# The head of full attention in a macaron block: query scale in the row masks, expert sums between the first scores, keys and values as jobs beside the first maxima

## The chip, the cores and the metric

The kernel runs on one core of a Trainium2 chip. The metric is the device time of one execution in microseconds. TensorE is called PE (PEld for its weight loads), VectorE DVE, ScalarE ACT, GpSimd POOL, SyncE SP. All data are fp32.

## The reference

Two "macaron" layers run one after the other on x of shape (2, 2048, 256), each as half a feed-forward block, attention, and half a feed-forward block, each with a layer norm in front:

```python
x = x + 0.5 * experts(layernorm(x))
x = x + attention0(layernorm(x))        # full: q = x@Wq.T * (1/16), 16 heads of 16
x = x + 0.5 * experts(layernorm(x))
x = x + 0.5 * recurrence(layernorm(x))
x = x + attention1(layernorm(x))        # causal, rotary, relative positions; q / 4
x = x + 0.5 * recurrence(layernorm(x))
```

`experts` sends each token to the 2 best of 6 experts (gated feed-forward blocks), adds the two results with their weights, and adds a shared block of the same form. `attention0` ends with `out @ Wff.T + bff`.

## The kernel before, in words

x (4096 tokens of 256) stays in SBUF as 32 chunks of 128 tokens; batch 0 is chunks 0 to 15, batch 1 chunks 16 to 31. The order of every engine's work is that of the program; nothing is reordered by a scheduler. PSUM is a ring of eight banks (`bank()`), taken in the order of the program by all products, so a product waits until whoever read the bank eight allocations before has done so.

**The expert stage** (`moe`) routes and sorts each batch's tokens, scatters them to DRAM (`places`) in the order of their experts, and runs the experts over tiles of 128 rows (`experts`), which go to DRAM again (`results`). Then `combine(h, c)` brings chunk c of batch h together: for each of the token's two experts POOL issues an indirect gather from `results` into a buffer `yg` (L435), and DVE multiplies it with its weight and adds it to x (L440, a scalar_tensor_tensor with two SBUF inputs). The sums of batch 0 are made while the experts run for batch 1. Those of batch 1 (16 chunks, 32 gathers and 32 sums) follow the experts, through `rest(n)`: n chunks at a time between the last products of the shared block (`up`, `mul`, `down`; L145, L336, L343). In the first expert stage no pool `gathered` is given: `yg` has 6 buffers in the stage's own pool, and `rest(HC)` makes all remaining sums before the stage ends. In the second it lies in a pool of its own with 12 buffers, and the remaining sums are called from `recurrence`.

**Full attention** (`attention0`) has 32 groups t of one batch, one block of 512 queries and 4 heads. The four heads of a group lie in rows 32j to 32j + 15 of the partitions, or, for odd groups, in rows 32j + 16 to 32j + 31. `queries(t)` makes one product for two groups and writes it twice, through `part_rows` (L138): an ACT activation whose scale is a column of the table `rowsel`, 1 in the rows that count and 0 in the others. `keys(b, g, qc)` does the same for the keys of two groups and one block of 512, with a bias column besides. `vals` makes the values of 8 heads for 512 keys (16 matmuls of 128 columns, L603, and an ACT copy, L609), after two small ACT writes that pad them (L620, L624).

`largest` computes 128 x 512 scores of one head (L757) and DVE takes their maximum per row (L761); 64 of these per group, then `mneg` (L764) holds the negative maxima. `subtract` puts them into the query's spare row. `exponential` computes scores turned over (L771), with ACT's Exp (L776). `weighted` multiplies them with the values (L783), four products per unit, which ACT copies out (L643) and POOL adds up (L541).

**The order around the change.** A step has two half steps, n = 0 and 1. A half step has 4 exponentials of one group interleaved with 4 maxima of a later group, then its half of the step's jobs, then one unit of `weighted`. Exponentials begin in step 9; in steps 0 to 7 only the first group's maxima run, in step 8 the second's first ones. Jobs are listed by step in `jobs`: `queries(0)` is due at step -2; at step -1 stand four `add_bias` (POOL adds the output bias to x of batch 0 in 128 x 1024 pieces, L587), the eight `keys` of batch 0's first and third group pairs, and its eight `vals`. Before any of these the attention scales the query weights with 1/16 on DVE (L721), and POOL clears two tiles (`mneg`, L555). In the later `recurrence` a similar DVE instruction scales the query weights of `attention1` with 1/4.

Of the kernel before, what the change touches and what calls it, by code (L numbers as in the profile page):

```python
# [17 lines left out]
P = 128  # L18
B = 2
S = 2048  # L20
D = 256
# [21 lines left out]
def macaron_kernel(ctx: ExitStack, tc: tile.TileContext, t: dict, out: bass.AP):  # L43
# [6 lines left out]
    nc.gpsimd.memset(mhalf, -0.5)  # L50


    rowsel = const.tile([P, 4], F32, name="rowsel")


    xpool = ctx.enter_context(tc.tile_pool(name="xpool", bufs=1))
# [109 lines left out]
    def moe(w, ws, gate_w, gate_b, rev, tri, iota, z, behind, last, gathered):  # L166
# [3 lines left out]
        with ExitStack() as s:  # L170
# [257 lines left out]
            def combine(h, c):  # L428

                for i in range(2):  # L430
                    yg = (wk if gathered is None else gathered).tile(
                        [P, D], F32, name="yg", bufs=6 if gathered is None else 12
                    )
                    k = i * HC + c
                    nc.gpsimd.indirect_dma_start(  # L435
                        out=yg, out_offset=None, in_=results[h],
                        in_offset=bass.IndirectOffsetOnAxis(ap=place[h][:, k : k + 1], axis=0),
                    )
                    xs = x[:, h * HC + c, :]
                    nc.vector.scalar_tensor_tensor(  # L440
                        xs, yg, weight[h][i][:, c, :], xs, ALU.mult, ALU.add
                    )
# [260 lines left out]
                skew.append(u)  # L703


    def attention0(norm, tail, wq, wk_, wv, wo, bff):

        with ExitStack() as s:
            z = Pieces(s, "a0", norm, wo, bff)
            kpool = pool(s, "a0_k", side="right")
            vpool = pool(s, "a0_v", side="right")
            wk, q = z.wk, z.q
            groups = [(b, qc, g) for b in range(B) for qc in range(SB) for g in range(G)]

            nc.vector.tensor_scalar_mul(wq, wq, 1.0 / 16.0)  # L721
            NG = len(groups)
            kT, v, mx = {}, {}, {}

            def keys(b, g, qc):

                pk = bank()
                mm2(pk, wk_, ts(g // 2, P), z.xnT(b, qc))
                for i in range(2):
                    if qc == 0:  # L730
                        kT[b, g + i] = kpool.tile([P, S], F32, name="kT", bufs=5)
                    part_rows(kT[b, g + i][:, ts(qc, TB)], pk, i, rowsel[:, 2 + i : 3 + i])

            vs = [vpool.tile([P, NKB, HV * VW + DH - 1], F32, name=f"v{n}") for n in range(3)]

            def vals(b, half, qc):
                if qc == 0:
                    v[b, half] = vs[(2 * b + half) % 3]
                if 2 * b + half < 3:
                    z.pad_values(vs[2 * b + half][:, ts(qc, CPB), :])  # L740
                z.values(v[b, half][:, ts(qc, CPB), :], wv, b, qc, half, None)

            def queries(t):

                b, qc, g = groups[t]
                pq = bank()
                mm2(pq, wq, ts(g // 2, P), z.xnT(b, qc))
                for i in range(2):
                    q[t + i] = wk.tile([P, TB], F32, name="q", bufs=4)
                    part_rows(q[t + i], pq, i, None)  # L750
                    mx[t + i] = wk.tile([P, CPB * J, SB], F32, name="mx", bufs=4)

            def largest(t, u, j):
                b, qc, g = groups[t]
                qb, kc = u // SB, u % SB
                ps = bank()
                nc.tensor.matmul(  # L757
                    ps, lhsT=q[t][rows(j), ts(qb, P)], rhs=kT[b, g][rows(j), ts(kc, TB)],
                    start=True, stop=True,
                )  # L760
                nc.vector.tensor_reduce(mx[t][:, qb * J + j, kc : kc + 1], ps, AX.X, ALU.max)  # L761
                if u == NKB - 1 and j == last_j:
                    m = z.mnegs[t % 2].rearrange("p a j r -> p (a j) r")
                    nc.vector.tensor_reduce(  # L764
                        m[:, :, z.row(t)], mx[t], AX.X, ALU.max, negate=True
                    )

            def exponential(t, kb, j):
                b, qc, g = groups[t]
                st = bank()  # L770
                nc.tensor.matmul(  # L771
                    st, lhsT=kT[b, g][rows(j), ts(kb, P)], rhs=q[t][rows(j), :],
                    start=True, stop=True,
                )
                z.pTs[t, kb, j] = wk.tile([P, TB], F32, name="pT", bufs=8)
                nc.scalar.activation(z.pTs[t, kb, j], st, AF.Exp)  # L776

            def weighted(t, kb):
                b, qc, g = groups[t]
                pv = bank()  # L780
                for j in range(J):
                    h = (g % 2) * J + j
                    nc.tensor.matmul(  # L783
                        pv[rows(j), :], lhsT=v[b, g // 2][:, kb, ds(h * VW, 32)],
                        rhs=z.pTs.pop((t, kb, j)), start=True, stop=True,
                    )
                z.gather(t, pv, 4)

            jobs = Jobs()
            at = jobs.at  # L790
            PER = 8
            for t in range(NG):
                at(PER * t + 8, z.subtract, t)
            for b in range(B):
                first = b * SB * G * PER

                for qc in range(SB) if b else ():
                    for c in range(CPB):
                        at(first - 43 + 4 * qc + c, z.ln_stats, b, qc, c)
                    at(first - 37 + 4 * qc, z.ln_transpose, b, qc)  # L800
                for qc in range(0 if b else SB):
                    norm.xn.pop(qc)
                    at(-1, z.add_bias, qc)
                for g in range(0, G, 2):
                    for qc in range(SB):
                        at(first - 7 + PER * g + qc if b else -1, keys, b, g, qc)
                for half in range(2):
                    for qc in range(SB):
                        due = first + 1 + 16 * half + qc
                        at(due if b else -1, vals, b, half, qc)  # L810
            for t, (b, qc, g) in enumerate(groups):
                if t % 2 == 0:
                    at(PER * t - 2, queries, t)
                at(PER * t + 18, z.divide, t, b, qc, g, True)
                if g == G - 1:
                    at(PER * t + 19, z.outputs_T, b, qc)
                    at(PER * t + 20, z.outputs, b, qc, 0)
                    at(PER * t + 20, z.outputs, b, qc, 1)

            at(60, fill_skew)  # L820
            for step, fn, *args in tail:
                at(PER * NG + step, fn, *args)
            for step in range(min(jobs), max(jobs) + 1):
                todo = jobs.get(step, [])
                for n in range(2):
                    z.begin(2 * step + n)
                    te, tm = (step - 9) // PER, step // PER
                    ke, um = ((step - 9) % PER) * 2 + n, (step % PER) * 2 + n
                    exps = 0 <= te < NG
                    last_j = 1 if exps else 3  # L830
                    for j in range(J):
                        if exps:
                            exponential(te, ke, j)
                        if 0 <= tm < NG:
                            largest(tm, um, (j + 2) % J if exps else j)
                    for fn, args in todo[n * (len(todo) + 1) // 2 :][: (len(todo) + 1 - n) // 2]:
                        fn(*args)
                    unit = 2 * (step - 9) + n - 1
                    if 0 <= unit < NG * NKB:
                        weighted(unit // NKB, unit % NKB)  # L840
            z.finish()
# [136 lines left out]
    def attention1(norm, tail, w, relk, relv, kbias, dramp, skew):  # L978
# [4 lines left out]
        with ExitStack() as s:  # L983
# [85 lines left out]

            def queries_out(t):  # L1070
                for i in range(2):
                    part_rows(q[t + i], q[t + 1], i, None)

            def by_position(t):

# [353 lines left out]
    with tc.manual_schedule(engines=ENGINES):  # L1429

        n0, n1, n2, n3, n4, n5 = (Norm() for _ in range(6))
        with ExitStack() as s:
# [9 lines left out]
            def loads0():  # L1442
                weights.extend(load(wp, n) for n in ("a0_q", "a0_k", "a0_v", "a0_o", "a0_b"))

            run_moe(n0, ahead.run, nothing, loads0, clear=True)
            tail = []
            for b in range(3):
                tail += [(1 + 2 * b, n2.stats, b), (2 + 2 * b, n2.normal, b, nc.vector),
                         (3 + 2 * b, n2.turn, b)]
            tail.append((7, n2.stats, 3))  # L1450
            attention0(n1, tail, *weights)


        with ExitStack() as s:
# [25 lines left out]
            def normals(cb):  # L1480

                if cb == 1:


                    nc.vector.tensor_scalar_mul(a["q"], a["q"], 0.25)
                    nc.vector.scalar_tensor_tensor(
                        kbias, rowsel[:, 0:2], rel0[:, 0:1], rowsel[:, 2:4], ALU.mult, ALU.add
                    )
# [22 lines left out]
def _layout(i):  # L1511
# [52 lines left out]

    rowsel = np.zeros((J, 2, DH, 4), f)
    for n in range(2):
        rowsel[:, n, :, n] = 1.0
        rowsel[:, 1 - n, 0, 2 + n] = 1.0  # L1570
    o["rowsel"] = rowsel.reshape(P, 4)
    o["rev"] = np.broadcast_to(np.arange(NE, 0, -1, dtype=f), (P, 1, NE))
    inv = (f(1.0) / f(10000.0) ** (np.arange(0, DH, 2, dtype=f) / f(DH))).astype(f)
    ang = np.outer(np.arange(S, dtype=f), inv).astype(f)
# [24 lines left out]
```

## Time and profile before

| what | value |
|---|---|
| median of 3 runs | 4118.79 us (4115.33 to 4121.76) |
| profiled execution, its own time | 4118.51 us |
| its span, first to last instruction | 4116.6 us |
| mean granted PE clock | 0.985 |
| PE busy | 4012.2 us, 97% of the span |
| DVE busy | 2702.9 us, 66% |
| ACT busy | 2570.1 us, 62% |
| POOL busy | 1634.7 us, 40% |
| gathers `yg<-results`, L435 | 128, 0.94 us each on POOL, data 2.8 us after issue (median) |
| sums `x<-yg`, L440 | 128, 0.48 us each (median), longest 9.84 us |
| maxima `mx<-s`, L761 | 2048, 0.68 us each |

A row of the timeline gives start, length, engine, line, operation and, in brackets, the idle time before it with what ended it. In rows of stretches, busy times of the engines are followed by the granted PE clock, as a share of full speed. "x" counts records; an fp32 matmul leaves two. Times of overlapping instructions are longer than their spacing: the maxima follow each other closer than 0.68 us apart.

### The profile page before, as it was taken

What the parts mean: (1) busy time and instruction counts of PE and PEld (TensorE: products, weight loads), DVE (VectorE), ACT (ScalarE), POOL (GpSimd) and SP (SyncE); (2) the same over time, 40 slices, a digit from 0 to 9 for tenths busy, and PEclk for the clock granted to TensorE, in tenths of its full rate; (3) what the DMA queues carried; (4) which work ended last, traced back from release to release, by engine and by line L of the source; (5) the groups of instructions that cost most, each with busy time, mean ns of one, the idle gap of its engine ahead of it and who ended that gap; (6) DMA issues with size and microseconds to landing.
All of it is one profiled execution on the core that took longest, in us unless ns stands there. A gap on an engine that the chain in (4) does not pass through costs nothing.

```text
span 4116.6 us, 76431 instructions
## 1 busy us (share of the span) xinstructions
PE 4012.2 (97%) x28256; PEld 1950.3 (47%) x28256; DVE 2702.9 (66%) x6130; ACT 2570.1 (62%) x5227; POOL 1634.7 (40%) x1456
## 2 busy tenths in 40 slices
PE   8996999999999999999999999999999999999999
PEld 4664533333334433333345654655554455554445
DVE  6243888888776788888843344666677756677533
ACT  2332488888887888888853322266667766667832
POOL 4244133336433333333344240245546655554410
PEclk9998899999999999999999999999999999999999
DMA  7341000100000000000023420154442334442101
GB/s 258 116 128 54 1 1 1 47 1 1 1 1 1 1 1 1 1 1 1 10 85 130 128 86 6 37 119 91 98 96 56 84 78 90 101 91 53 45 22 41
DMA packets 355508, 223.18 MB, mean 54 GB/s; under 512 B 146624, under 2 KB 338496, under 8 KB 355136
## 3 DMA queue, kind: packets, MB, share of 16 engines
q1 hardware_dynamic: 276800, 176.33, 16.3%
q0 software_dynamic: 12288, 33.57, 2.6%
q10 hardware_dynamic: 66048, 8.39, 1.3%
q8 instruction: 225, 3.69, 0.4%
q14 instruction: 147, 1.20, 0.1%
HBM read 113.12 MB, written 105.12 MB: 53 GB/s over the span
## 4 chain that ended last, share of the span: by engine, by line
PE 90%; DVE 5%; POOL 2%; ACT 1%; issue 1%; DMA 1%; SPq 0%; POOLq 0%; DVEq 0%; ACTq 0%
PE s L771 13%; PE s L783 12%; PE s L757 10%; PE s L145 10%; PE s L1236 7%; PE s L382 6%; PE s L1122 6%; PE s L1207 6%; PE s L402 3%; PE s L680 1%; PE s L603 1%; PE s L1221 1%; PE s L1200 1%; PE s L343 1%; PE s L1217 1%
## 5 line engine op out<-in xcount | busy, mean ns | idle before, releaser
L541 POOL TENSOR_TENSOR part<-part 128x512 f32<-128x512 f32 (+3 forms) x800 | 962.8, 1204 | 1436.3 <-ACT part L643 1428.2
L761 DVE TENSOR_REDUCE mx<-s 128x1 f32<-128x512 f32 x2048 | 1270.1, 683 | 327.4 <-PE s L757 327.2
L776 ACT ACTIVATE pT<-s 128x512 f32<-128x512 f32 x2048 | 1063.7, 617 | 236.5 <-PE s L757 234.5
L757 PE MATMUL s<-kT,q 32*128 32x512 f32 x4096 | 1033.6, 630 | 0.0
L771 PE MATMUL s<-q,kT 32*128 32x512 f32 x4096 | 1013.3, 615 | 0.0
L1228 ACT ACTIVATE pT<-s 128x512 f32<-128x512 f32 (+3 forms) x1280 | 587.5, 541 | 252.1 <-PE s L1207 103.9
L771 PEld LDWEIGHTS s<-q,kT 32*128 32x128 f32 x4096 | 417.8, 183 | 465.9 <-DVE mx L761 327.0
L643 ACT COPY part<-s 128x512 f32<-128x512 f32 (+3 forms) x864 | 507.0, 588 | 148.9 <-PE s L783 60.1
L1130 DVE TENSOR_REDUCE mx<-s 128x1 f32<-128x512 f32 (+1 forms) x768 | 472.9, 679 | 131.1 <-PE s L1122 122.7
L783 PE MATMUL s<-pT,v 128*32 128x512 f32 x4096 | 549.8, 605 | 0.4 <-ACT pT L776 0.2
L757 PEld LDWEIGHTS s<-kT,q 32*128 32x128 f32 x4096 | 426.1, 187 | 127.5 <-ACT pT L776 76.5
L1122 PE MATMUL s<-kT,q 32*128 32x512 f32 (+7 forms) x2240 | 331.3, 433 | 0.0
L1236 PE MATMUL s<-pT,v 128*32 128x512 f32 (+3 forms) x2560 | 304.6, 541 | 11.4 <-DVE mx L1130 5.0
L382 PE MATMUL s<-we,xT 128*128 x592 | 278.7, 593 | 0.5 <-ACT xT L377 0.5
L389 DVE TENSOR_TENSOR h<-sg,s 128x256 f32<-128x256 f32 x148 | 62.3, 421 | 282.6 <-ACT sg L387 282.6
L1122 PE MATMUL s<-b,q 32*128 32x512 f32 (+7 forms) x1280 | 242.2, 516 | 1.6 <-DVE v L611 1.4
L783 PEld LDWEIGHTS s<-pT,v 128*32 128x32 f32 x4096 | 82.1, 108 | 336.0 <-ACT pT L776 300.3
L1146 DVE CUSTOM_DVE_ANT_0 band<-s,band 128x160 f32<-128x160 f32 (+1 forms) x512 | 155.7, 314 | 129.0 <-PE s L1207 62.8
L541 POOL TENSOR_TENSOR band<-band,mneg 128x640 f32<-128x640 f32 x128 | 161.3, 1261 | 190.0 <-DVE mneg L1156 130.4
L1207 PE MATMUL s<-q,kT 32*128 32x512 f32 (+3 forms) x1152 | 235.6, 508 | 0.0
L435 POOL DMA_INDIRECT yg<-results,at x128 | 123.4, 964 | 241.0 <-DMA results<-y 117.4
L1207 PE MATMUL s<-q,b 32*128 32x512 f32 (+3 forms) x896 | 208.2, 568 | 0.0
(229 smaller groups left out, 5147.2 us busy)
## 6 DMA issues: line engine op xcount, KB each, us to landing
band<-skew SPq DMA_DIRECT2D x32, 1280.0 KB, 7.9
pd<-band SPq DMA_DIRECT2D x32, 1280.0 KB, 9.3
xs<-places SPq DMA_DIRECT2D x148, 128.0 KB, 2.3
results<-y SPq DMA_DIRECT2D x148, 128.0 KB, 1.7
places<-zero SPq DMA_DIRECT2D x2, 4736.0 KB, 21.3
we<-in_we SPq DMA_DIRECT2D x12, 768.0 KB, 8.7
skew<-s ACTq DMA_DIRECT2D x32, 256.0 KB, 3.0
s<-pd SPq DMA_DIRECT2D x32, 256.0 KB, 4.8
```

The source lines that it names most:

```text
L382: nc.tensor.matmul(pu, lhsT=xT[n][:, ts(kc, P)], rhs=w[:, kc, ds(val[n], 2 * D)], start=kc == 0, stop=kc == 1,)
L541: fn(*args)
L643: nc.scalar.copy(part[:, q0:], pv[:, q0:])
L757: nc.tensor.matmul(ps, lhsT=q[t][rows(j), ts(qb, P)], rhs=kT[b, g][rows(j), ts(kc, TB)], start=True, stop=True,)
L761: nc.vector.tensor_reduce(mx[t][:, qb * J + j, kc : kc + 1], ps, AX.X, ALU.max)
L771: nc.tensor.matmul(st, lhsT=kT[b, g][rows(j), ts(kb, P)], rhs=q[t][rows(j), :], start=True, stop=True,)
L776: nc.scalar.activation(z.pTs[t, kb, j], st, AF.Exp)
L783: nc.tensor.matmul(pv[rows(j), :], lhsT=v[b, g // 2][:, kb, ds(h * VW, 32)], rhs=z.pTs.pop((t, kb, j)), start=True, stop=True,)
L1122: nc.tensor.matmul(ps[:, ds(cols, n)], lhsT=lhsT, rhs=kT[b, c, g][rows(j), ds(k0, n)], start=True, stop=True,)
L1207: nc.tensor.matmul(ps[:, q0:], lhsT=k, rhs=q[t][rows(j), q0:], start=True, stop=True, skip_group_check=True,)
L1228: nc.scalar.activation(z.pTs[t, kb, j][:, q0:], st.pop((t, kb, j))[:, q0:], AF.Exp)
L1236: nc.tensor.matmul(pv[rows(j), q0:], lhsT=v[b, kb // CPB, g // 2][:, kb % CPB, ds(h * VW, 32)], rhs=z.pTs.pop((t, kb, j))[:, q0:], start=T ...
```

## The change

Four things are done.

The scales 1/16 and 1/4 are no longer multiplied into the query weights on DVE. `rowsel` has four more columns, 1/16 and 1/4 in the rows that count, and the queries of both attentions use these in `part_rows`.

The first expert stage is given a pool `gathered` too, so that `moe` returns with eight chunks of batch 1 not yet summed. `attention0` calls `rest(1)` at the end of each half step of steps 0 to 3: two gathers on POOL, which stand there behind the four `add_bias`, and two sums on DVE, behind the half step's four maxima. `yg` has 10 buffers in both stages.

Of batch 0's keys only the first pair's four blocks stay at step -1. The other pair's blocks are jobs of steps 0 to 3, one a step.

Of batch 0's values nothing stays at step -1: eight jobs, one in each of steps 0 to 7.

```diff
-    rowsel = const.tile([P, 4], F32, name="rowsel")
+    rowsel = const.tile([P, 8], F32, name="rowsel")
...
                     yg = (wk if gathered is None else gathered).tile(
-                        [P, D], F32, name="yg", bufs=6 if gathered is None else 12
+                        [P, D], F32, name="yg", bufs=6 if gathered is None else 10
                     )
...
-    def attention0(norm, tail, wq, wk_, wv, wo, bff):
+    def attention0(norm, tail, rest, wq, wk_, wv, wo, bff):
...
-            nc.vector.tensor_scalar_mul(wq, wq, 1.0 / 16.0)
...
-                    part_rows(q[t + i], pq, i, None)
+                    part_rows(q[t + i], pq, 4 + i, None)
...
-                        at(first - 7 + PER * g + qc if b else -1, keys, b, g, qc)
+                        at(first - 7 + PER * g + qc if b else (qc if g else -1), keys, b, g, qc)
                 for half in range(2):
                     for qc in range(SB):
-                        due = first + 1 + 16 * half + qc
-                        at(due if b else -1, vals, b, half, qc)
+                        due = first + 1 + 16 * half + qc if b else 4 * half + qc
+                        at(due, vals, b, half, qc)
...
                     for fn, args in todo[n * (len(todo) + 1) // 2 :][: (len(todo) + 1 - n) // 2]:
                         fn(*args)
+                    if step in range(4):
+                        rest(1)
...
-                    part_rows(q[t + i], q[t + 1], i, None)
+                    part_rows(q[t + i], q[t + 1], 6 + i, None)
...
-            run_moe(n0, ahead.run, nothing, loads0, clear=True)
+            rest = run_moe(
+                n0, ahead.run, nothing, loads0, clear=True, gathered=pool(s, "gathered")
+            )
...
-            attention0(n1, tail, *weights)
+            attention0(n1, tail, rest, *weights)
...
-                    nc.vector.tensor_scalar_mul(a["q"], a["q"], 0.25)
...
-    rowsel = np.zeros((J, 2, DH, 4), f)
+    rowsel = np.zeros((J, 2, DH, 8), f)
     for n in range(2):
         rowsel[:, n, :, n] = 1.0
         rowsel[:, 1 - n, 0, 2 + n] = 1.0
-    o["rowsel"] = rowsel.reshape(P, 4)
+        rowsel[:, n, :, 4 + n], rowsel[:, n, :, 6 + n] = 1.0 / 16.0, 1.0 / 4.0
+    o["rowsel"] = rowsel.reshape(P, 8)
```

## Prediction

> **What bounds the kernel now.** I read the page first, then the stretch in which the first expert stage hands over to full attention, because every edit but two lies there. PE is busy 97% of the span, so only places where PE stands still, or is held to the pace of another engine, can give time. The busy times by stretch, then the chain of work that ended last:
>
> ```profile
> 349.00:373.00 24.00, 0.00 (x0) 0.00 (x0) 10.80 (x23) 0.00 (x0) 17.59 (x19) 0.57 0.33 98
> 373.00:384.00 11.00, 0.00 (x0) 0.00 (x0) 10.66 (x3) 0.00 (x0) 9.80 (x6) 0.50 0.04 13
> 384.00:390.00 6.00, 5.91 (x7) 2.52 (x8) 0.00 (x0) 1.27 (x2) 0.00 (x0) 0.50 0.01 3
> 390.00:417.00 27.00, 27.00 (x162) 19.84 (x160) 0.00 (x0) 18.10 (x39) 0.00 (x0) 1.00 0.00 1
> 418.00:424.00 6.00, 6.00 (x29) 2.74 (x22) 5.91 (x10) 0.94 (x1) 0.00 (x0) 1.00 0.00 0
> 424.00:456.00 32.00, 32.00 (x105) 25.30 (x102) 32.00 (x55) 0.00 (x0) 0.00 (x0) 0.50 0.00 1
> ```
>
> The columns are stretch, length, busy PE, PEld, DVE, ACT, POOL, granted clock, DMA. Three phases follow each other with no overlap: 35 us in which PE is empty, 33 us in which DVE is empty, and 38 us in which DVE is full and ACT empty.
>
> ```profile
> 373.25 9.85 DVE x L440
> ...
> 383.61 0.35 DVE a_q L721
> ...
> 384.09 18.62 PE s L145 x36
> 402.72 14.29 PE s L603 x128
> 417.01 1.11 PE s L757 x8
> 418.12 38.35 DVE mx L761 x64
> ```
>
> The chain shows the order: expert sums (L440), the query scale (L721), one query and eight key products (L145), eight value products (L603), then the first group's 64 maxima (L761). The timeline and the scale's row say who holds whom:
>
> ```profile
> 371.69 0.94 POOL L435 DMA_INDIRECT yg<-results,at  x1 [0.30 <-issue]
> ...
> 373.25 10.36 DVE L440 SCALAR_TENSOR_TENSOR x<-yg,col,x 128x256 f32<-128x256 f32 x2 [0.73 <-DMA yg<-results,at]
> 373.58 9.22 POOL L587 TENSOR_TENSOR x<-x,a_b 128x1024 f32<-128x1024 f32 x4
> 383.53 0.42 DVE L721 TENSOR_SCALAR a_q<-a_q 128x512 f32<-128x512 f32 x1
> ...
> 384.09 3.75 PE L145 MATMUL s<-b,a_q 128*128 128x512 f32 x4 [35.42 <-DVE a_q L721]
> ```
>
> PE's 35.42 us wait ends with the scale, which stands on DVE behind 32 expert sums; those come at the pace of POOL's gathers, 1.25 us apart, and the next to last sum lasts 9.85 us instead of 0.48, across POOL's four bias additions.
>
> **Query scale in the masks.** The 0.42 us on DVE goes, and with it PE's wait. In the changed program's order the first query product waits for ACT alone. Its mask product on ACT is the same instruction with another scale column, 0.64 us as now. The mask writes into reused memory and waits for the gpsimd DMA queues, but for counts that the early scatters reach. So PE goes on at 348.7, where its last shared-expert product (L343) ends, with a full clock. One query and four keys have four records each (two matmuls, each recorded twice); from 391.8 on, at full clock, the timeline has 25 such records in 10.89 us, 0.43 each, 1.72 a product. So 5 × 1.72 = 8.6, to 357.3. The first maxima's inputs could be there at about 358. The second scale (attention with positions, 0.25) took 0.42 us on a DVE that waits there in any case: 0 to −0.4, I take 0.
>
> **Expert sums moved.** Sixteen gathers stay ahead of the attention, sixteen come behind the bias additions on POOL. The buffers are now 10 where the first stage had 6, so gathers 13 and 15 lose their 0.8 and 1.1 us waits for DVE: the sixteenth starts at 330.97 + 15 × 1.25 = 349.7, POOL is done with it and two memsets (1.0) at 352, with the bias additions (9.2) at 361.2. The sixteenth sum's data lands at 349.7 + 2.8 = 352.5, inside the additions, so I let it be held as its twin was: to 361.2, and DVE is free at 361.8. What is queued behind it: all maxima, and through PSUM, PE, which by then has seven products ready.
> Here a rule speaks otherwise. The Trainium skill ("SBUF — State Buffer", on the engine ports) says that DVE with two SBUF inputs and GpSimd take a shared pair as an exclusive lock, and that whichever starts first keeps it for the whole instruction. The row has the sum starting 0.33 us before POOL and still lasting until all four additions were over. By the rule the sum would wait for one addition at most, DVE would be free near 355, and the maxima would start at 358. I take the row; but the sum differs little: the first pair of moved sums stands behind the first four maxima, and its gathers stand behind the additions on POOL in both readings. They start at 361.5 and 362.75, land 2.8 later, and the second sum ends at 365.55 + 0.5 = 366.05 either way.
> From there a half step has four maxima (38.35 / 64 = 0.60 each, 2.4) and two sums (0.48 each, 1.0): 3.4 us against 2.5 for two gathers, so gathers no longer bind. Seven more half steps: 7 × 3.4 = 23.8, to 389.9. Eight half steps without sums: 19.2, to 409.1. Before, the 64th maximum ended at 418.12 + 38.35 = 456.5. Difference **47.4 us**. Of the 16 sums' 7.7 us on DVE nothing is hidden; it is in this figure.
>
> **Keys and values as jobs.** Four key products (1.72 PE each, 1.45 ACT) and eight value products (14.29 / 8 = 1.79 PE, 1.1 ACT) move out of the chain, 21.2 us of PE, into the maxima. ACT was empty there. For PE: four weighted products, eight records, take 1.0 us in the steady chain, and I use that for four maxima. Steps 0 to 3 need 2 × 1.0 + 1.72 + 1.79 = 5.5 at full clock, against 6.8 of DVE; steps 4 to 7 need 3.8 against 4.8. At half clock 11.0 and 7.6: 4 × 4.2 + 4 × 2.8 = 28 us beyond DVE. So the cover is there at full clock and is gone at half. Which clock?
> The Trainium skill ("TensorE: Matmul & The Clock Gate", why this matters) says the clock stays up while there are no PE gaps over about 3 us. The rows of 418 to 456 disagree: PE waited for DVE by fractions of a microsecond only, some 40% loaded (1.0 of 2.4), and was at 0.50 from 424 on. By the rule the excess would be 0; if load decides as in that row, up to 28. The new load is 80%, nearer the full rows (1.00 at 390 to 417) than the 40% one, and a PE that falls to half clock becomes saturated and rises again, as at 384 to 390, within 6 us. I take 1 us of excess and keep 28 for the range. A warm PE also shortens the step after the maxima, which now runs at 0.50 until 461: four transposes 1.11 and eight records 2.02 would halve, −1.5.
>
> **Buffers 12 to 10 in the second expert stage.** There gathers run 1.25 apart and sums follow some 3 us later, so at most about five buffers are out: 0, at worst 2. The wider rowsel load (8 columns) is behind the x loads: 0.
>
> **Sum.** −47.4 + 1 − 1.5 + 0.9 for a jitter of half a gather and the POOL gaps (0.3 each) = −47. The profiled execution took 4118.5 us around a span of 4116.6; the median of the three runs is 4118.8, so both bases agree: 4118.8 − 47 = **4072**.
>
> **Rivals.**
> *A, DVE sets the pace* (the sum above): 4064 to 4080, chance 0.62. For it: DVE at 32.00 of 32.00 and ACT at 0 in the maxima.
> *B, PE becomes the bound at half clock.* It costs 8 to 28 us: 4080 to 4100, middle 4088. For it: the 0.50 over 32 us in which PE never stood still long. Against: the higher load. Chance 0.29.
> *C, the change does not reach its aim*: PE's queue meets another old wait, such as the bank freed by the last shared-expert sums, and starts near 384 again. Then only the products moved into the maxima count, and even these lose to sums on DVE: about 21 − 8 = 13 us less. That gives 4106, and with the clock of B no change, 4119. The program's order speaks against it: the bank's DVE release is at 349.4. Chance 0.05, of it 0.03 within 0.2%.
> *D, slower.* One mechanism: PE's clock does not come back when the exponentials start, in step 9. Each half step of the steady part takes 2.93 us at full clock and would take 5.9 at half; from the 16th such half step on, the 47 us are lost, so 0.50 until beyond about 500 would make it slower, at 40 half steps 4142. Against it: now the clock rises from 0.50 to 1.00 within 4 us of the first exponentials. Chance 0.04.
>
> **How the numbers follow.** About 0.2% (8 us) is what a measurement of this kernel can tell from no change. Faster: A 0.62, B 0.29 and 0.02 of C, 0.93; same 0.03; slower 0.04. The range is A's with most of B: 4064 to 4092. The low end is −47 with the whole step after the maxima warm, the first sum not held, and DVE pausing nowhere; the high end is half of B's cost and a little more.
>
> **What would show it.** Right: PE without a gap from 348.7 to about 358; the first maxima near 358 to 362; a sum of over 8 us next to the bias additions still there; the 64th maximum near 409; PE clock mostly 1.00 between 362 and 409. Wrong: clock 0.50 through that stretch with DVE waiting for PE (B); PE idle ahead of the first query (C); a half step with sums of well over 3.4 us, which would mean that gathers and two-input sums get in each other's way.

## The result

| kernel, on the same chip | median | lowest to highest |
|---|---|---|
| before | 4117.06 us (4 runs) | 4110.78 to 4121.76 |
| after | 4068.96 us (4 runs) | 4067.63 to 4069.54 |

The ratio is 0.9886, 95% interval 0.9871 to 0.9900: some 48 us less. The profiled execution of after took 4068.88 us around a span of 4067.0; before it was 4118.51 around 4116.6. So the profiled pair differs by 49.6 us in span, and this is the difference that the following rows must account for.

The busy times by stretch, for after (columns as before: stretch, length, PE, PEld, DVE, ACT, POOL, granted clock, DMA share, GB/s):

```profile
344.00:362.00 18.00, 16.46 (x56) 8.13 (x54) 16.26 (x14) 8.78 (x14) 16.29 (x13) 1.00 0.15 45
...
364.00:366.00 2.00, 2.00 (x14) 2.00 (x12) 1.69 (x5) 0.00 (x0) 1.39 (x3) 0.59 0.28 86
...
372.00:390.00 18.00, 18.00 (x115) 10.91 (x115) 17.82 (x33) 6.41 (x16) 6.81 (x7) 1.00 0.21 60
...
408.00:412.00 4.00, 3.60 (x16) 1.37 (x20) 4.00 (x7) 0.00 (x0) 0.00 (x0) 0.59 0.00 0
```

The three phases of before, each with one engine empty, are gone: from 344 on PE, DVE and ACT have work at the same time, and from 372 on PE and DVE are both full (to 406). The chain of work that ended last, for after (start, length, engine, tile and line):

```profile
340.92 6.92 PE s L344 x32
...
350.82 1.24 DVE x L441
352.06 8.65 issue
...
361.93 2.78 DMA yg<-results,at
...
378.49 2.48 DVE mx L760 x4
380.96 0.40 DVE x L441
...
388.49 19.15 DVE mx L760 x32
...
407.74 0.22 DVE mneg L763
```

Where before had PE pieces for keys (18.62 us) and values (14.29 us) between the sums and the maxima, there is none now: the path goes from sums to maxima on DVE alone. The 8.65 us called issue, after a sum that the chain cuts to 1.24 us, are the rest of the sum that lasts until the bias additions are over, so DVE's 16.26 us of 344 to 362 are mostly this hold; the timeline has it whole:

```profile
347.66 1.88 PE L146 MATMUL s<-b,a_q 128*128 128x512 f32 x4
...
350.82 9.97 DVE L441 SCALAR_TENSOR_TENSOR x<-yg,col,x 128x256 f32<-128x256 f32 x1
351.24 9.26 POOL L588 TENSOR_TENSOR x<-x,a_b 128x1024 f32<-128x1024 f32 x4
...
361.62 2.48 DVE L760 TENSOR_REDUCE mx<-s 128x1 f32<-128x512 f32 x4
...
362.36 1.12 PE L756 MATMUL s<-kT,q 32*128 32x512 f32 x2 [1.90 <-DVE mx L760]
```

PE takes the first query product where the last shared-expert product leaves it, with no wait in brackets. That the rest of the program only follows earlier is read from the first and last start of `mneg`, of which there is one per group. For before, then for after (least, median and greatest length in ns, then the first and the last start):

```profile
L764 DVE TENSOR_REDUCE mneg<-mx x32: 221/222/222, 456.6 to 2052.3; 128x16 f32<-128x64 f32 x32
L1156 DVE TENSOR_REDUCE mneg<-mx x128: 161/168/177, 2658.2 to 3868.7; 128x4 f32<-128x8 f32 x32, 128x4 f32<-128x12 f32 x32, 128x4 f32<-128x16 f32 x32, 128x4 f32<-128x20 f32 x24
```

```profile
L763 DVE TENSOR_REDUCE mneg<-mx x32: 221/222/223, 407.7 to 2002.9; 128x16 f32<-128x64 f32 x32
L1157 DVE TENSOR_REDUCE mneg<-mx x128: 160/168/178, 2608.9 to 3818.9; 128x4 f32<-128x8 f32 x32, 128x4 f32<-128x12 f32 x32, 128x4 f32<-128x16 f32 x32, 128x4 f32<-128x20 f32 x24
```

So the first group is 48.9 us earlier, the last group 49.4, the other attention's first 49.3, its last 49.8: all of the gain is there when the first maxima end, and nothing is given back.

### The profile page after: what moved, and what is told of

Read it like the earlier page. It is cut to its first block, busy times and chain, and to the rows that moved or that the text cites. A ratio compares the mean times of both kernels' runs of the same rounds, so it can differ in the third digit from the quotient of the medians.

```text
span 4067.0 us, 76436 instructions
## 1 busy us (share of the span) xinstructions
PE 3996.5 (98%) x28256; PEld 1930.7 (47%) x28256; DVE 2701.9 (66%) x6128; ACT 2568.8 (63%) x5227; POOL 1634.8 (40%) x1456
## 4 chain that ended last, share of the span: by engine, by line
PE 90%; DVE 5%; POOL 1%; ACT 1%; issue 1%; DMA 0%; SPq 0%; POOLq 0%; ACTq 0%; DVEq 0%
PE s L770 13%; PE s L782 12%; PE s L756 10%; PE s L146 10%; PE s L1237 7%; PE s L1123 6%; PE s L383 6%; PE s L1208 6%; PE s L403 3%; PE s L681 2%; PE s L1222 1%; PE s L1201 1%; PE s L1218 1%; PE s L344 1%; PE s L931 1%
## 5 line engine op out<-in xcount | busy, mean ns | idle before, releaser
L756 PE MATMUL s<-kT,q 32*128 32x512 f32 x4096 | 1018.6, 618 | 1.9 <-DVE mx L760 1.9
L756 PEld LDWEIGHTS s<-kT,q 32*128 32x128 f32 x4096 | 406.4, 184 | 128.9 <-ACT pT L775 76.2
## 6 DMA issues: line engine op xcount, KB each, us to landing
we<-in_we SPq DMA_DIRECT2D x12, 768.0 KB, 11.6
```

Of the source, the lines that this page charges most:

```text
L756: nc.tensor.matmul(ps, lhsT=q[t][rows(j), ts(qb, P)], rhs=kT[b, g][rows(j), ts(kc, TB)], start=True, stop=True,)
```

## The experiments

Each kernel differs from after, or from before where that is said. The first four shared one chip (before: 4118.12 us, close to the 4117.06 of the result, so the two are called the first chip here). Jobs alone, bias later, two keys and steady sums shared a second, the last four runs a third; on these every kernel takes some 115 to 140 us longer (before: 4232.65 and 4232.90 us), so each is compared within its own chip.

### The scale alone: before with only the scale in the masks

```diff
-            nc.vector.tensor_scalar_mul(wq, wq, 1.0 / 16.0)
...
-                    part_rows(q[t + i], pq, i, None)
+                    part_rows(q[t + i], pq, 4 + i, None)
...
```

(Left out here: the wider table, and the 1/4 of the other attention, which goes into the masks in the same way.)

> The kernel before with the query scale in the masks and nothing else. Theory T (two arms meet at the first maximum: PE's products and DVE's sums; the later one sets it): PE starts its 29.8 us of products at 348.7 and is done at 378.5, DVE's last sum still ends at 383, so the first maximum moves from 418.1 to 383.2, about -35 us, 4084 in all; the maxima phase keeps its 38.4 us and a clock of 0.50. Rival R (each of the three edits brings a share of its own, and they add up): sums 12 and jobs 21 of the 48 us are theirs, 15 are left for the scale, 4103.

Measured: 4084.11 us (4082.88 to 4086.74) against 4118.12, ratio 0.9920 (0.9903 to 0.9936). Its timeline:

```profile
373.93 10.43 DVE L440 SCALAR_TENSOR_TENSOR x<-yg,col,x 128x256 f32<-128x256 f32 x2 [0.72 <-DMA yg<-results,at]
...
384.27 2.48 DVE L760 TENSOR_REDUCE mx<-s 128x1 f32<-128x512 f32 x4
```

PE starts its query at 349.2 here too, and its first score products end at 380.2, before DVE is free: the last pair of sums is held beside the bias additions (POOL, from 374.28), and the maxima follow it at once, with no wait in brackets. The gain is there at the first `mneg` (424.0 instead of 456.6) and about the same at the last one of the other attention (3835.8 instead of 3868.7), so it is the 1/16 that gives it and not the 1/4. Removing that one instruction of 0.42 us gives 34 us, because PE's products no longer stand behind the sums but run beside them. What is left is DVE's own line, as the theory had it, and PE's is only 4 us shorter.

### The scale back: after with 1/16 on DVE again

```diff
+            nc.vector.tensor_scalar_mul(wq, wq, 1.0 / 16.0)
...
-                    part_rows(q[t + i], pq, 4 + i, None)
+                    part_rows(q[t + i], pq, i, None)
```

> The changed kernel with the 1/16 of full attention multiplied into the query weights on DVE again. T: PE waits until DVE leaves the sum that is held by the bias additions, about 362, and then needs a query and four keys, 8.6 us at full clock and some 2.5 more on a PE that has fallen to 0.50; first maximum near 373 instead of 361.6, +12 us against the changed kernel, 4081. R: the scale's share of 15 is lost, 4084. The two differ little here; the profile tells whether PE's wait ends with the scale near 362.

Measured: 4079.11 us (4076.47 to 4082.89), ratio 0.9908 (0.9892 to 0.9925), by the medians 10 us more than after. The intervals of the two ratios just overlap, so the timeline has to decide:

```profile
361.31 0.42 DVE L721 TENSOR_SCALAR a_q<-a_q 128x512 f32<-128x512 f32 x1
361.88 3.75 PE L146 MATMUL s<-b,a_q 128*128 128x512 f32 x4 [14.31 <-DVE a_q L721]
...
374.20 2.48 DVE L761 TENSOR_REDUCE mx<-s 128x1 f32<-128x512 f32 x4 [12.47 <-PE s L757]
```

The scale comes right after the sum that the bias additions hold up, PE waits 14.31 us for it, and then DVE waits 12.47 us for PE: sums and products are in series again. The first `mneg` is 12.3 us later than in after (420.0 and 407.7), the last one of the other attention 10.1 (3829.0 and 3818.9).

### No jobs: after with all first keys and values ahead of the maxima

```diff
-                        at(first - 7 + PER * g + qc if b else (qc if g else -1), keys, b, g, qc)
+                        at(first - 7 + PER * g + qc if b else -1, keys, b, g, qc)
...
-                        due = first + 1 + 16 * half + qc if b else 4 * half + qc
-                        at(due, vals, b, half, qc)
+                        due = first + 1 + 16 * half + qc
+                        at(due if b else -1, vals, b, half, qc)
```

> The changed kernel with all keys and values of batch 0 back in front of the first maxima; scale in the masks and moved sums stay. T: products end near 377.5, first maximum at 378, then 38.4 + 7.7 us on DVE, 64th maximum near 424 against 407.6, 4086: the moved sums bring nothing over the scale alone, as PE's arm is now the later one. R: 15 + 12 are gained, 4091.

Measured: 4088.26 us (4082.33 to 4091.53), ratio 0.9925 (0.9908 to 0.9941). The first maxima of its timeline:

```profile
379.41 2.48 DVE L760 TENSOR_REDUCE mx<-s 128x1 f32<-128x512 f32 x4 [16.94 <-PE s L756]
```

DVE is free early, as in after, but its line now waits 16.94 us for PE's products. The median lies between the two theories' figures; the first maxima at 379.4 and the bracket show the mechanism.

### No moved sums: after with all sums ahead of the attention

```diff
-                    if step in range(4):
-                        rest(1)
...
+            rest(HC)
             attention0(n1, tail, rest, *weights)
```

> The changed kernel with all sixteen chunks summed ahead of the attention, as before; scale in the masks and jobs stay. T: DVE's arm is the later one, first maximum at 383 as with the scale alone, no sums beside the maxima, 64th near 421.5, 4084: the jobs bring nothing over the scale alone. R: 15 + 21 are gained, 4082. With the products beside maxima that follow each other without sums, 2.4 us a half step, PE needs 2.75 a half step in steps 0 to 3 even at full clock: a further +3 if that holds, more if the clock falls.

Measured: 4084.81 us (4083.17 to 4087.43), ratio 0.9922 (0.9905 to 0.9938): no gain over the scale alone, though 21 us of PE products are now beside the maxima. The time alone cannot tell the two theories apart (4084 and 4082); the timeline shows what happens:

```profile
380.56 4.87 DVE L760 TENSOR_REDUCE mx<-s 128x1 f32<-128x512 f32 x8
381.31 2.07 PE L756 MATMUL s<-kT,q 32*128 32x512 f32 x2 [21.51 <-DVE mx L760]
...
388.07 2.48 DVE L760 TENSOR_REDUCE mx<-s 128x1 f32<-128x512 f32 x4 [2.63 <-PE s L756]
...
391.05 2.48 DVE L760 TENSOR_REDUCE mx<-s 128x1 f32<-128x512 f32 x4 [0.50 <-PE s L756]
```

PE stands still for 21.5 us, since DVE holds its banks; then the products that became jobs come at PE's pace, 2.98 us from one half step's maxima to the next (388.07, 391.05), where DVE alone needs 2.4. The phase from the first maxima to `mneg` lasts 45.6 us (380.6 to 426.2), as long as the 46.1 us of after (361.6 to 407.7), which has sixteen sums in it besides.

So the gains don't add up:

| in the kernel | gain against before beside it |
|---|---|
| scale | 34 us |
| scale and jobs | 33 us |
| scale and moved sums | 30 us |
| jobs and moved sums | 39 us |
| all three | 48 us |

Moved sums without the other two edits were not run; jobs alone follow below, on another chip. Two lines meet at the first maxima, PE's products and DVE's sums, and the later one counts. With the scale alone they end at 380 and 384; the jobs shorten only the first, the moved sums only the second, and either alone leaves the other where it was (first maxima at 380.6 and 379.4). Only with both do they start at 361.6. In the maxima it is the same: the jobs make PE's half step 3.0 us, the sums make DVE's 3.3, and the two lie beside each other.

### Jobs alone: before with only keys and values as jobs

```diff
-                        at(first - 7 + PER * g + qc if b else -1, keys, b, g, qc)
+                        at(first - 7 + PER * g + qc if b else (qc if g else -1), keys, b, g, qc)
...
-                        due = first + 1 + 16 * half + qc
-                        at(due if b else -1, vals, b, half, qc)
+                        due = first + 1 + 16 * half + qc if b else 4 * half + qc
+                        at(due, vals, b, half, qc)
```

> The kernel before with the second keys and the values as jobs and nothing else; scale on DVE and all sums ahead. T: PE starts at 384 at half clock for 6 us, first maximum near 395; steps 0 to 3 are set by PE, 2.98 us a half step as seen without sums beside the maxima, steps 4 to 7 by DVE: 8 x 2.98 + 8 x 2.4 = 43, 64th maximum near 438.5 instead of 456.5, -18, 4100. R (the jobs' share of the sum is what they take out of the chain): -21, 4097; the profile tells which half steps PE sets.

Measured on the second chip: 4221.05 us (4216.21 to 4226.28) against 4232.65, ratio 0.9973 (0.9963 to 0.9984), 11.6 us less. The two pieces are near those of T: from query to first maxima 12.0 us (11 expected), then 44.2 us from the first maxima to `mneg` (449.3 to 493.5; 43 expected) where before on the first chip had 38.5: of the 21 us moved out of the path, some 6 come back there, as PE sets the pace of the maxima. That would leave 15; where the other 3 to 4 went has no row, since before left no profile on this chip. The total is short of both forecasts (18 and 21).

### Two ways to shorten what is left

In after the first maxima still wait for the held sum. **Bias additions later** makes them jobs of steps 4 to 7, behind the moved sums. **Two keys** does that and leaves only two key blocks ahead of the maxima:

```diff
-                    at(-1, z.add_bias, qc)
+                    at(4 + qc, z.add_bias, qc)
...
-                        at(first - 7 + PER * g + qc if b else (qc if g else -1), keys, b, g, qc)
+                        at(first - 7 + PER * g + qc if b else (1 + qc if g else (qc > 1) - 1), keys, b, g, qc)
...
-                        due = first + 1 + 16 * half + qc if b else 4 * half + qc
+                        due = first + 1 + 16 * half + qc if b else 1 + 4 * half + qc
```

(The first edit alone is the bias kernel; all three are the keys kernel.)

> The changed kernel with the four bias additions as jobs of steps 4 to 7 instead of step -1, so that POOL's gathers stand ahead of them. T with the hold (the two-input sum is held by POOL's additions, maxima that read PSUM are not): no sum over 1 us is left, DVE is free near 353, the first maximum is set by PE's query and four keys, 357.3 for a query at 347.7 instead of 361.6, gathers no longer bind; -4.5 us, 4064.5. Rival (the long sum was no hold by the additions but late data): nothing changes, 4069. Rival (additions hold maxima too): 9 us are lost in steps 4 to 7, 4074.

> As e5, and only two of the first pair's four key blocks stay ahead of the first maximum; the other two become jobs of step 0, and the second pair's keys and the values move one step later (1 to 4, 1 to 8). T (PE's arm is now the later one): two products of 1.72 us less ahead of the first maximum, which comes near 353.8; -8 us against the changed kernel, 4061. Rival (DVE is not free before about 357, or PE waits for ACT's masks in the first half steps): no more than e5, 4064.5.

On the second chip: 4201.36 us (4198.36 to 4209.38), ratio 0.9929 (0.9917 to 0.9941), and 4201.42 (4200.31 to 4205.90), ratio 0.9930 (0.9917 to 0.9943). After itself had not run on that chip, so all three were run together on a third:

> The changed kernel once more, unchanged, as the measure for the three beside it on the same chip: a ratio to the kernel before of 0.9886 as at first (0.987 to 0.990); on a chip on which engines wait for other reasons too, the same 48 us in a longer time.

> The bias additions as jobs of steps 4 to 7, a second time, beside the changed kernel. T with the hold: 4.5 us under the changed kernel of the same call, no sum over 1 us, first maximum 9.6 us after the first query's start instead of 13.9. Where DVE is late for another reason, as in the first run of this kernel, the additions come to stand beside sums again and hold one of them for their 9 us.

> Two key blocks ahead of the first maximum, a second time, beside the changed kernel. T: 8 us under the changed kernel, first maximum 6.1 us after the first query's start. Rival: no more than the bias additions alone, 4.5.

After took 4205.57 us (4197.07 to 4207.57), ratio 0.9936 (0.9922 to 0.9949); bias later 4205.01 (4198.37 to 4209.14), 0.9934 (0.9921 to 0.9948); two keys 4201.69 (4198.03 to 4207.54), 0.9929 (0.9916 to 0.9943). Neither gain is shown, and after's own gain is only 27 us here. The waits of after on the third chip (engine, tile and line, releaser: us in total, times, longest) between 395 and 480:

```profile
DVE x L349 <- remote: 6.4, 1, 6.4
...
ACT kT L139 <- remote: 5.1, 1, 5.1
```

Remote is a releaser outside of what the trace of this core can name; on the first chip neither before nor after has such a wait. These stalls of DVE and ACT lie ahead of and within the very work that the edits move. And the bias additions met sums again, as the timeline of bias later on the third chip shows:

```profile
435.77 9.23 POOL L588 TENSOR_TENSOR x<-x,a_b 128x1024 f32<-128x1024 f32 x4
...
438.43 2.48 DVE L760 TENSOR_REDUCE mx<-s 128x1 f32<-128x512 f32 x4 [4.76 <-remote]
...
440.83 4.98 DVE L441 SCALAR_TENSOR_TENSOR x<-yg,col,x 128x256 f32<-128x256 f32 x2
```

The first maxima came 11.6 us after the query in both kernels (9.6 and 6.1 expected), against 18.1 in after on this chip. But the phase from the first maxima to `mneg` grew to 59.4 us with the bias later and 61.2 with two keys, against 53.2, so what was gained ahead of the maxima was lost within them. In part that is the hold once more: POOL, which runs ahead of a stalled DVE, reached the additions while sums were still to come, and the pair of sums ends with the additions. In the two-keys kernel one sum is held for 7.64 us in the same way. The four maxima in between, which read PSUM, keep their 2.48 us beside the same additions. Whether the edits pay on the first chip was not tried.

### Sums in the steady part

The next kernel moves the sums out of the first maxima altogether, a pair to every second step from 12 to 26, on top of the two-keys kernel (the other keys come every second step then):

```diff
-                    if step in range(4):
+                    if step in range(12, 28, 2) and n:
                         rest(1)
```

> As e6, with the eight chunks' gathers and sums moved on into the steady part, one chunk in every second step from 12 to 26, and the second pair's keys spread over steps 1, 3, 5, 7. T: the maxima of the first group lose the 7.7 us of sums; PE needs 2.3 us a half step on the mean, DVE 2.4; in the steady part DVE is busy 84% and has room for 0.5 us a half step; -15.5 us against the changed kernel, 4053.5. Rival (sums of two SBUF inputs are held by POOL's additions of parts, 1.2 us in each 2.9, and the maxima behind them hold PE): up to 1.2 us for each of 16 sums comes back, 4061 to 4073.

Measured on the second chip: 4223.21 us (4217.26 to 4226.94), ratio 0.9977 (0.9968 to 0.9986): 22 us slower than the two-keys kernel, where the theory had 7.5 us less than that kernel and the rival 0 to 12 more. The maxima phase shrank to 41.9 us, but from the first to the last weighted product it took 1669.3 us, against 1635.6 in the two-keys kernel, 34 us more. Its timeline at one of the pairs:

```profile
495.82 2.17 DVE L441 SCALAR_TENSOR_TENSOR x<-yg,col,x 128x256 f32<-128x256 f32 x1 [1.47 <-DMA yg<-results,at]
499.13 0.48 DVE L441 SCALAR_TENSOR_TENSOR x<-yg,col,x 128x256 f32<-128x256 f32 x1 [1.14 <-DMA yg<-results,at]
499.53 2.48 DVE L760 TENSOR_REDUCE mx<-s 128x1 f32<-128x512 f32 x4
500.27 1.21 PE L770 MATMUL s<-q,kT 32*128 32x512 f32 x1 [3.67 <-DVE mx L760]
```

A sum waits for a gather that was issued just before it; DVE, which works in order, cannot go on with the maxima; PE then stands still 3.67 us for a bank, and its clock is 0.50 from 500 to 506. The sixteen sums wait 15.9 us for data in all. The rival cause is that sums are held beside POOL's work: the one at 495.82 lasts 2.17 us, eight others 0.62 to 1.08, together 5.7 us more than sixteen undisturbed ones. One more kernel takes the waits for data away: the sums stand in the same stretch, one per step instead of a pair every second step, and their gathers are issued at half steps 0 to 4 (31, 35 and 39 for the last three pairs), long ahead.

```diff
-                    if step in range(4):
-                        rest(1)
+                    if 2 * step + n in (0, 1, 2, 3, 4, 31, 35, 39):
+                        rest.fetch()
+                    if n and step in range(12, 28):
+                        rest.add()
```

(`fetch` issues one chunk's two gathers, `add` makes one sum.)

> As two keys, but the sums of the eight chunks go one at a time into steps 12 to 27 of the steady part, while their gathers are issued long before (five chunks beside the first maxima, three when buffers come free), so that no sum waits for data; the second pair's keys are spread over steps 1, 3, 5, 7. With the gathers issued next to the sums, the same place had cost 35 us in the steady part. T (there DVE stood in line waiting for data, and PE for DVE's maxima): that cost goes, and the first maxima lose 7.7 us of sums; about -12 to -15 us against the changed kernel. Rival (holds by POOL's additions are what costs): the steady part is still 20 us or more longer than with the changed kernel.

Measured on the third chip: **4183.17 us** (4182.75 to 4191.49) against 4232.90, ratio 0.9889 (0.9873 to 0.9904). Beside it, after has 0.9936 (0.9922 to 0.9949): the intervals do not meet, and this kernel is the faster one by 22 us. The sums of its trace, and PE and DVE in the maxima:

```profile
L442 DVE SCALAR_TENSOR_TENSOR x<-yg,col,x x128: 472/483/519, 268.2 to 2541.1; 128x256 f32<-128x256 f32 x128
```

```profile
419.00:430.00 11.00, 10.24 (x56) 4.44 (x50) 9.16 (x16) 4.06 (x8) 8.84 (x9) 1.00 0.36 108
430.00:445.00 15.00, 15.00 (x104) 9.25 (x100) 14.57 (x25) 4.67 (x12) 7.91 (x4) 1.00 0.01 1
```

No sum of all 128 is held any more (longest 0.52 us), none in the steady part waits for data, the clock there stays at 0.99 to 1.00 (475 to 1000), and from first to last weighted product it takes 1635.5 us (after on this chip: 1634.0). So the 34 us are not the price of sixteen sums in this stretch as such, but of gathers issued right ahead of them. The expected rival, that the holds remain and cost 20 us or more, is not what happened, but the holds went together with the waits and the pairs became single sums. What each of these would cost alone (15.9 us of waiting and 5.7 us of longer sums in the trace, and PE's half clock behind them) is not separated.

The profiled executions of after and of this kernel differ by 13.7 us in span, less than the medians. This kernel's query starts 1.7 us later (407.8 and 406.1); then it gains 6.5 us between query and first maxima (11.6 and 18.1) and 11.3 between first maxima and `mneg` (41.9 and 53.2); some 2 of these 16 us are gone at the end. How much of the gain depends on the remote stalls of this chip is open: on the first chip after's figures were 14.0 and 46.1, and this kernel did not run there.

## Why the prediction was right

It said 4072 us, and 4068.96 was measured. By its steps:

**PE goes on without a gap: right.** The query starts at 347.66; 348.7 had been said. Why PE reached the place 1 us earlier is not shown. From the query to the first score product (356.34) it took 8.7 us; 8.6 had been said.

**First maxima near 358 to 362, behind a held sum: right, and the row was a better guide than the rule.** The sum started at 350.82, the first addition at 351.24, and the sum lasted 9.97 us, across all four additions. The rule of the Trainium skill ("SBUF — State Buffer", on the engine ports), that the first starter keeps the lock for its instruction, would have ended it after 0.5 us, if the recorded starts are those that count. POOL's memsets, which also run at that time (350.28 to 351.29), are no explanation: the sum before, at 350.30, took its usual 0.48 us beside them. One detail was different. Held was the 14th of the 16 sums, which started before the additions, and not the 16th, whose data would land among them; the last two followed at 360.71 and 361.22. The end of the hold is the same in both cases, so the figure did not suffer. Maxima began at 361.62.

**Half steps of 3.4 us, gathers not binding: right, a little long.** Second sum's end 365.28 (366.05 said), then seven half steps of four maxima and two sums up to 388.49, 3.31 us each (3.4 said), then 19.15 us for the rest (19.2 said). The 64th maximum ended at 407.64; 409.1 had been said. Before it was 456.5, so the term is −48.8 instead of −47.4.

**PE's cover: right in sign, thinner than worked out.** PE's half step was put at 2.75 us in steps 0 to 3. The experiment without moved sums shows 2.98, so DVE's 3.31 leaves 0.3 to spare. The 1 us of excess was not spent.

**The clock: mostly right.** It is 1.00 from 344 to 364 and from 368 to 408, so rival B did not come. But it fell to 0.59 at 364 to 366 and 0.56 in the next 2 us, after PE had stood still for only 1.90 us, which cost nothing since DVE set the pace, and to 0.59 between 408 and 412. So the −1.5 us for a warm step after the maxima was not earned: from the 64th maximum to the first weighted product it is 9.1 us, before 9.5. The rule of the Trainium skill ("TensorE: Matmul & The Clock Gate", why this matters), that the clock stays up as long as no PE gap exceeds about 3 us, is not what these rows show.

**Buffers 12 to 10: right at 0.** From the last group of this attention to the end nothing more is lost: 49.4 us earlier there, 49.6 at the end.

**The sum.** −48.8 at the 64th maximum, −0.4 up to the first weighted product, −0.4 in all the rest: −49.6 for the profiled pair. The prediction's −47 had errors of 1 to 2 us that partly cancel, so a part of the close agreement is luck: 1.4 too little up to the maxima, 1.1 too much for the warm step (1.5 said, 0.4 found), and 1.9 of excess and jitter that did not come; 0.4 of the rest has no row.

Rivals: C (PE starts late) is excluded by the query at 347.66, D by the last `mneg`, which kept the whole gain. D's figure was also wrongly added up: 40 half steps at 2.93 us more each are 117 us on top of 4072, 4189 and not 4142, which would be 24 half steps. Nothing else rests on it. What the prediction did not see is how far its parts depend on each other; it added them along one path and never asked what each gives alone, where any two of the three give 30 to 39 us and the scale alone already 34.

## What to carry to other kernels

Where three phases follow each other with a different engine empty in each, look for the one small instruction that ties them: here 0.42 us on DVE cost 34 us, because PE's whole queue stood behind it. Where two lines meet at one point, the later one sets it, so a part tried alone tells little about what it is worth with the others: price every part with the rest in place. On an engine that works in order, issue a gather well ahead of the instruction that uses it: sixteen sums in the same stretch cost 34 us with fresh gathers, in pairs, and nothing with early ones, one at a time.

## What was not expected of the hardware

- The granted clock fell below 0.6 for about 4 us after PE gaps of 1.90 and 1.59 us. A gap does not decide it alone: in the kernel with early gathers a gap of 1.69 us (PE waiting for ACT until 415.33) left the clock at 1.00. What does is open.
- A DVE sum with two SBUF inputs is held until the whole run of POOL's four bias additions is over, even where by the recorded starts it was first (by 0.42 us here, 9.97 us long). These additions leave no gap: each starts 0.04 to 0.07 us before the recorded end of the one ahead. Where two additions of POOL are 0.08 us apart (497.69 and 497.77, with sums in the steady part), a waiting sum ended at 497.99, while the second one ran. That the gap lets it in fits these cases but was not tested. DVE maxima out of PSUM pass beside the same additions at full pace (2.48 us for four).
- On two other chips the same programs take longer (before 4232.65 and 4232.90 us against 4118.12; after, on the third, 4205.57 against 4068.96), with waits of DVE and ACT for remote releasers of up to 15 us each. On the third, the change gains 27 us instead of 48. What releases these waits was not found.
